# Two hybrid layers on one core: the last batch in halves of positions, its gated jobs in tiles, and query projections moved ahead

## The chip, the core and the metric

The kernel runs on one core of a Trainium2 chip. Its engines each work through an instruction queue of their own, in order, and wait for one another by semaphores: PE (TensorE, matrix multiplication and transposes through it), DVE (VectorE), ACT (ScalarE), POOL (GpSimd), and SP, which here only issues DMAs. Matrix results land in PSUM, in banks of 128 partitions by 512 float32; everything else lies in SBUF.

The metric is the device time of one launch in microseconds (us), as the median of several runs. The profile is one further execution, recorded by the hardware profiler. Its "span" is the time from the first to the last instruction.

## What is computed

The input x has 4 batches of 512 positions and 256 features, all in float32. Four blocks follow each other, each added to x:

```python
x = x + _L0_attn_a_ref(_layernorm(x), ...)   # full attention, 16 heads of 128
x = x + _L0_ffn_ref(_layernorm(x), ...)      # gated job, below
x = x + _L0_attn_b_ref(_layernorm(x), ...)   # low-rank attention, 16 heads
x = x + _L0_ffn_ref(_layernorm(x), ...)      # gated job again
```

The low-rank attention compresses x to 64 columns, projects queries (and a rotary part of 64) from them, scores causally, and multiplies back:

```python
q = x @ Wqa @ Wqb;  ckv = x @ Wkva
attn = softmax(where(causal, concat(q_nope, rope(q_pe)) @ concat(k_nope, rope(k_pe)).T * scale, min))
out = (attn @ v).reshape(b, n, H * VDIM) @ Wout
```

The gated job (`_L0_ffn_ref`) transposes the first two axes: it runs along the batch index l (4 steps), separately for each of the 512 positions. At step l it needs the normalised x of step l-1 (a convolution of width 2) and the keys and values of all steps up to l, but nothing of other positions:

```python
x = silu(x_prev * conv_w[:, 0] + x * conv_w[:, 1])
q, k, v, g = silu(x @ Wq), x @ Wk, x @ Wv, x @ Wg    # q, k rotated by l
qk = (q_exp @ k_exp.T) * HDK ** -0.5 * tril            # 4 x 4 over l, 16 heads
out = (silu(g) * headwise_norm(qk @ v)) @ Wout
```

## The kernel before

**Tiles and jobs.** A batch of x is four SBUF tiles `x[b][t]` of 128 positions. Two attention loops set the order of the PE work. Beside them run "jobs": Python generators that issue a few instructions and then yield. They stand in two lanes, `norms` (layer norms, L132) and `work` (mainly `gated`, L525), and `beside(times)` (L125) advances them by that many steps, alternating between the lanes. There is no scheduler: the order in which the program issues instructions is the order on each engine. A gated job of one batch is two generators, one for each half (two tiles, `HT` = 2), taken in turn (`in_turn`, L731).

**First attention** (`attention_full`, L180). One unit is one head of one batch: scores (L288), maximum (L296), exponential (L299), division by the sum on POOL (L314), a transpose by way of DRAM (`carry`, L328: one DMA out, four DMAs back, all from SP's queue), values (L350), output projection (L372). In the last units `prologue(i)` and `prologue_end(i)` (L1088, L1109) issue the start of the second attention: stage -3 loads rotary tables and query weights (`load_tables`), stage -2 loads the key weights (`load_keys`) and compresses the queries, stage -1 compresses the keys (L944) and projects query pair 0 (L977), stage 0 projects pairs 1 to 3 (pair 1 already stands at the end of stage -1).

**Second attention** (`attention_lowrank`, L845). One unit is (batch b, octet of heads o, half s of the octet, query tile t): four heads by 128 queries, as four blocks of 32 queries (index i). There are 64 units, 16 to a batch, and t runs fastest: 0, 1, 2, 3. Tile t sees (t+1)*128 keys, so units of t = 2, 3 have wide instructions. `score(u, i)` is one matmul (L1000), the masked maximum on DVE (L1008) and the exponential on ACT (L1011). `divide(u)` is a reciprocal (L1024) and four POOL multiplications (L1027). `turn(u, k)` is four PE transposes (L1035), whose copy out is on ACT (L1044), or on DVE for k = 1 of the wide units (L1042). `values(u, k)` multiplies by the values (L1059). `output(b, o, t)` projects four heads back and adds to x (L1079, L1086). `project` fills `queries` for one head pair: two matmuls, two DVE products, a shuffle, two ACT copies and two POOL additions (`rotated`, L906).

In the loop (L1120) unit u's slot i holds, in this order, values of unit u-3, score of unit u, turns of unit u-2 and, in slot 0, the division of unit u-1; then projections and outputs at fixed places, and last

```python
                    beside(beside_at[j % NT][i] * (1 if b < B - 1 else 2))
```

which is 16 steps for four units, and 32 in the last batch.

**The gated jobs' places.** `during_lowrank` (L1200) adds the norm and the gated job of batch b-1 (second layer) in unit 4 of batch b. After the loop, L1214 empties the lanes. Then the norm of batch 3 (all four tiles) runs, and its gated job as two halves in turn, each output tile stored by a DMA (L1216 to L1218).

Of the kernel before, what the change touches and what calls it, by code (L numbers as in the profile page):

```python
# [19 lines left out]
P = 128  # L20
# [16 lines left out]
def network(ctx: ExitStack, tc: tile.TileContext, ins: dict, out: bass.AP):  # L37
# [94 lines left out]
    def norm(b, take, extra=None):  # L132
# [3 lines left out]
        for t in range(NT):  # L136
            nc.vector.bn_stats(stats[:, t, :], x[b][t])
            nc.vector.bn_aggr(mv[:, t, :], stats[:, t, :])
            yield
        rstd = lnpool.tile([P, NT], F32, name="rstd")  # L140
        nc.gpsimd.tensor_scalar(rstd, mv[:, :, 1], EPS, None, ALU.add)
        nc.gpsimd.tensor_tensor(rstd, rstd, minus_half[:, :NT], ALU.pow)
        shift = lnpool.tile([P, NT], F32, name="shift")
        nc.gpsimd.tensor_tensor(shift, mv[:, :, 0], rstd, ALU.mult)
        nc.gpsimd.tensor_scalar(shift, shift, -1.0, 1.0, ALU.mult, ALU.mult)
        yield
        yield
        xT = new_xT()
# [15 lines left out]
        for t in range(0, NT, 2):  # L164
            normed = [normalise(t), normalise(t + 1)]
            if extra and t + 2 == NT:
                extra()
            yield
            for i in range(2):
                transpose(t + i, normed[i])  # L170
            yield
# [353 lines left out]
    def gated(layer, l, xT, xT_before, half, after):  # L525


        tiles = range(half * HT, (half + 1) * HT)
        rows = slice(half * HT * P, (half + 1) * HT * P)

        def little(name, cols, tag=None):
            return gpool.tile([P, cols], F32, tag=f"{tag or name}_{half}", name=name)


        cx = wide("cx", half).rearrange("p (c s) -> p c s", c=DC)
# [11 lines left out]
        th = wide("w0", half, "th").rearrange("p (c s) -> p c s", c=DC)  # L547
# [4 lines left out]
        q = wide("q", half).rearrange("p (t k) -> p t k", t=HT)  # L552
        kv = wide(f"kv{l}", half, "kv").rearrange("p (t k) -> p t k", t=HT)
        gd = wide("gd", half).rearrange("p (t k) -> p t k", t=HT)
        for i in range(HT):
# [19 lines left out]
        def rotate(a):  # L575

            qk = a.rearrange("p t (a f j) -> p t a f j", f=2, j=HDK // 2)
            part = [P, HT, H, HDK // 2]
# [4 lines left out]
            size = HT * H * HDK // 2  # L583
            tmp = [
                turn_tmp[:, i * size : (i + 1) * size].rearrange("p (t a j) -> p t a j", t=HT, a=H)
# [12 lines left out]
        thq = wide("w0", half, "thq", HT * DK).rearrange("p (t k) -> p t k", t=HT)  # L598
        thg = wide("w1", half, "thg").rearrange("p (t v) -> p t v", t=HT)
        nc.scalar.activation(thq, q, AF.Tanh, scale=0.5)  # L600


        r = little("r", HT * H, f"r{l}")
        by_tile = [r[:, i * H : (i + 1) * H] for i in range(HT)]
        nc.vector.tensor_scalar(r.rearrange("p (t h) -> p t h", t=HT), dl, -(2.0**-25), None, ALU.is_ge)
        history[layer, l, half] = kv, r
        gap = little("gap", HT * H)
        nc.vector.scalar_tensor_tensor(
            gap.rearrange("p (t h) -> p t h", t=HT), dl, -1.0, dl, ALU.mult, ALU.max
# [4 lines left out]
        e = gpool.tile([P, B, HT * H], F32, tag=f"e_{half}", name="e")  # L614
        for m in range(l + 1):
            nc.vector.tensor_tensor(e[:, m], r, history[layer, m, half][1], ALU.is_equal)
# [7 lines left out]
        count = little("count", HT * H)  # L624
        if l:
            nc.vector.tensor_reduce(count, e[:, : l + 1].rearrange("p m h -> p h m"), AX.X, ALU.add)
        else:
# [11 lines left out]
            e[:, : l + 1], e[:, : l + 1], gap.unsqueeze(1).to_broadcast([P, l + 1, HT * H]), ALU.mult  # L639
# [4 lines left out]
        a = gpool.tile([P, B, HT * H], F32, tag=f"a_{half}", name="a")  # L644
        prod = wide("w0", half, "prod").rearrange("p (i t k) -> p i t k", i=2, t=HT)
        for m in range(l + 1):
            nc.vector.tensor_tensor(prod[:, m % 2], q, history[layer, m, half][0][:, :, :DK], ALU.mult)
            nc.vector.tensor_reduce(
                a[:, m], prod[:, m % 2].rearrange("p t (h d) -> p (t h) d", d=HDK), AX.X, ALU.add
            )  # L650
            yield
        nc.vector.tensor_tensor(a[:, : l + 1], a[:, : l + 1], e[:, : l + 1], ALU.mult)
        yield
        o = wide("cx", half, "o").rearrange("p (t v) -> p t v", t=HT)
        part = [o] + [
            wide(f"w{i}", half, "part").rearrange("p (t v) -> p t v", t=HT) for i in range(min(l, 2))
        ]

        def weigh(engine, to, m):
            engine.tensor_tensor(  # L660
                to.rearrange("p t (h d) -> p t h d", d=HDV),
                history[layer, m, half][0][:, :, DK:].rearrange("p t (h d) -> p t h d", d=HDV),
                a[:, m].rearrange("p (t h) -> p t h", t=HT).unsqueeze(3).to_broadcast([P, HT, H, HDV]),
# [20 lines left out]
        sq = wide("w0", half, "sq").rearrange("p (n d) -> p n d", d=HDV)  # L684
        nc.scalar.activation(sq, og, AF.Square)
        yield
        var = little("var", HT * H)
# [4 lines left out]
        half_var, root = little("half_var", HT * H, "gap"), little("root", HT * H)  # L692
        square = little("square", HT * H, "count")
# [11 lines left out]
        nc.vector.tensor_tensor(og, og, root.unsqueeze(2).to_broadcast([P, HT * H, HDV]), ALU.mult)  # L705
        yield
        oT = wide("w1", half, "oT").rearrange("p (t n) -> p t n", t=HT)
        pt = ps_tp()
        for i in range(HT):
# [135 lines left out]
    def attention_lowrank(xTs, events):  # L845
# [5 lines left out]
        units = [(b, o, s, t) for b, o in octets for s in range(2) for t in range(NT)]  # L851
        n, per_batch = len(units), OCT * 8
# [7 lines left out]
        def load_tables():  # L860
            angles, wq = slot("wv1", "angles"), slot("wv0", "wqb")
            nc.sync.dma_start(angles, tables[:, : 2 * S])
            nc.sync.dma_start(wq, to_queries)
# [3 lines left out]
            lw["wq"] = wq.rearrange("r (o p s k) -> r o p s k", o=OCT, p=4, s=2)  # L867
# [38 lines left out]
        def rotated(first, second, ps):  # L906
# [5 lines left out]
                slot(tag, "turns").rearrange("p (i q) -> p i q", q=32)  # L912
                for tag in ("wq0", "wk1")
# [54 lines left out]
        def project(b, o, p):  # L968

            if p == 0:  # L970
                queries[b, o] = [
                    slot(tag, f"qTb{s}").rearrange("p (i h q) -> p i h q", h=4, q=32)
                    for s, tag in enumerate((("probs0", "queries")[o % 2], f"v{o % 2}"))
# [72 lines left out]
        quads = {}  # L1046
# [3 lines left out]
        def values(u, k):  # L1050
# [15 lines left out]
            if k == t:  # L1066
                if t == 1:
                    quads[b, o, s] = slot(f"zT{1 + u // NT % 3}", "zTb").rearrange(
                        "p (t n) -> p t n", t=NT
                    )  # L1070
                nc.vector.tensor_copy(
                    quads[b, o, s][:, t - 1 : t + 1, :].rearrange("p b n -> p (b n)"), open_bank.pop()
                )

        def output(b, o, t):

            po = ps_mm()
            for i in range(4):
                nc.tensor.matmul(  # L1079
                    po[:, :D],  # L1080
                    lhsT=quads[b, o, i // 2][:, t, (i % 2) * P : (i % 2 + 1) * P],
# [6 lines left out]
        def prologue(i):  # L1088

            stage = i - H * B  # L1090
            if i == H * (B - 1):
                load_first()
            elif stage == -3:
                load_tables()
            elif stage == -2:
                load_keys()
                compress_queries(0)
            elif stage == -1:
                compress_keys(0)
                project(0, 0, 0)()  # L1100
            elif stage == 0:
                buffers()
                halves = [split(f"squares{k}", k) for k in range(2)]
                project(0, 0, 2)()
                probs_of(0, halves)
                probs_of(2, [slot("probs_2", "probs2")])
                probs_of(3, [slot("probs1", "probs3")])

        def prologue_end(i):  # L1109
            if i - H * B in (-1, 0):  # L1110
                project(0, 0, 3 + 2 * (i - H * B))()

        pair_at = {(1, 0): 0, (3, 1): 1, (5, 0): 2, (6, 1): 3}
        output_at = {(1, 1): 0, (1, 3): 1, (3, 0): 2, (3, 3): 3}
# [185 lines left out]
```

## Time and profile before

| what | us |
|---|---|
| median of 3 runs (lowest, highest) | 1459.04 (1457.69, 1462.09) |
| the profiled execution, its own time | 1464.73 |
| its span | 1463.0 |
| PE busy in the span | 1331.4 (91%) |
| DVE busy | 875.0 (60%) |
| ACT busy | 601.8 (41%) |
| POOL busy | 519.1 (35%) |

The second attention starts with the scores at 821.12 us of the span. Its batches begin there and at 964.92, 1097.40 and 1226.94 us. The last x is written by it at 1394.95 us. From there to 1463.0 us only the norm and the gated job of batch 3 run.

In a row of the timeline the first number is the start, the second the duration, both in us; then engine, line, operation, output and inputs with shapes, how many instructions ("x4"). In brackets stands how long the engine was idle before, and what ended the idle time. A float32 matmul is recorded as two passes, so "x8" on PE are four matmuls.

### The profile page before, as it was taken

What the parts mean: (1) busy time and instruction counts of PE and PEld (TensorE: products, weight loads), DVE (VectorE), ACT (ScalarE), POOL (GpSimd) and SP (SyncE); (2) the same over time, 40 slices, a digit from 0 to 9 for tenths busy, and PEclk for the clock granted to TensorE, in tenths of its full rate; (3) what the DMA queues carried; (4) which work ended last, traced back from release to release, by engine and by line L of the source; (5) the groups of instructions that cost most, each with busy time, mean ns of one, the idle gap of its engine ahead of it and who ended that gap; (6) DMA issues with size and microseconds to landing.
All of it is one profiled execution on the core that took longest, in us unless ns stands there. A gap on an engine that the chain in (4) does not pass through costs nothing.

```text
span 1463.0 us, 17042 instructions
## 1 busy us (share of the span) xinstructions
PE 1331.4 (91%) x4984; PEld 768.1 (53%) x4984; DVE 875.0 (60%) x2634; ACT 601.8 (41%) x1654; POOL 519.1 (35%) x907
## 2 busy tenths in 40 slices
PE   7989999999999999999998789988999999788852
PEld 3445555555656555565554555544555555445531
DVE  3544454553665647655467655698566765867537
ACT  3433333343343343333333246455565645453420
POOL 2311112221232223312144435575353535645333
PEclk9999999999999999999999799999999999898975
DMA  3686655643554445545344200000000000000000
GB/s 112 177 252 191 183 165 183 194 144 119 173 166 147 139 121 157 175 136 169 115 141 147 65 15 1 1 1 1 1 1 1 1 11 4 1 15 1 15 0 14
DMA packets 88140, 133.80 MB, mean 91 GB/s; under 512 B 16112, under 2 KB 69872, under 8 KB 88048
## 3 DMA queue, kind: packets, MB, share of 16 engines
q1 hardware_dynamic: 88048, 132.72, 30.5%
q8 instruction: 40, 0.66, 0.2%
q14 instruction: 52, 0.43, 0.1%
HBM read 86.29 MB, written 46.40 MB: 91 GB/s over the span
## 4 chain that ended last, share of the span: by engine, by line
PE 72%; DVE 13%; POOL 5%; ACT 4%; DMA 3%; issue 2%; SPq 1%; ACTq 0%; DVEq 0%; POOLq 0%
PE ps_mm L262 14%; PE ps_pz L350 8%; PE ps_sc L288 8%; PE ps_mm L249 7%; PE ps_mm L372 7%; PE ps_mm L559 6%; PE ps_sc L1000 5%; PE ps_pz L1059 4%; PE ps_mm L1079 3%; PE ps_tp L1035 3%; PE ps_mm L719 2%; DVE ps_sc L1008 2%; DMA way<-squares 2%; PE ps_mm L977 1%; POOL probs L1027 1%
## 5 line engine op out<-in xcount | busy, mean ns | idle before, releaser
L314 POOL TENSOR_SCALAR probs<-probs,inv 128x128 f32<-128x128 f32 (+3 forms) x256 | 135.1, 546 | 549.7 <-DVE inv L311 487.5
L299 ACT ACTIVATE probs<-ps_sc,nmax 128x128 f32<-128x128 f32 (+3 forms) x256 | 135.0, 528 | 268.6 <-DVE nmax L296 268.1
L1000 PE MATMUL ps_sc<-kTb,qTb 128*128 128x160 f32 (+15 forms) x512 | 175.5, 437 | 11.7 <-POOL qTb L923 5.1
L1011 ACT ACTIVATE probs<-ps_sc,nmax 128x160 f32<-128x160 f32 (+2 forms) x192 | 104.0, 542 | 199.1 <-DVE nmax L1008 138.3
L1008 DVE CUSTOM_DVE_ANT_0 ps_sc<-ps_sc,mask_b 128x32 f32<-128x32 f32 (+15 forms) x256 | 112.9, 444 | 91.4 <-PE ps_sc L1000 70.5
L288 PE MATMUL ps_sc<-kT,qT 128*128 128x128 f32 (+3 forms) x512 | 159.3, 434 | 1.9 <-DVE kT L276 0.9
L296 DVE CUSTOM_DVE_ANT_0 ps_sc<-ps_sc,mask_a 128x128 f32<-128x128 f32 (+3 forms) x256 | 126.3, 499 | 41.9 <-PE ps_sc L288 40.7
L350 PE MATMUL ps_pz<-probsT,v 128*128 128x512 f32 (+3 forms) x512 | 151.1, 438 | 0.0
L1027 POOL TENSOR_SCALAR probs<-probs,inv 128x160 f32<-128x160 f32 (+2 forms) x192 | 107.9, 580 | 109.5 <-DVE inv L1024 78.7
L1000 PEld LDWEIGHTS ps_sc<-kTb,qTb 128*128 128x128 f32 x512 | 84.8, 199 | 105.9 <-issue 58.9
L350 PEld LDWEIGHTS ps_pz<-probsT,v 128*128 128x128 f32 x512 | 97.6, 192 | 79.2 <-issue 58.2
L363 DVE TENSOR_SCALAR zT<-ps_pz,bias 128x512 f32<-128x512 f32 x64 | 48.0, 751 | 144.7 <-PE ps_pz L350 144.7
L262 PE MATMUL ps_mm<-xT,wk 128*128 128x512 f32 x256 | 124.3, 609 | 8.7 <-DMA wk<-in_a_wk_dram 8.5
L249 PE MATMUL ps_mm<-wv,xT 128*128 128x512 f32 x256 | 121.8, 601 | 0.0
L372 PE MATMUL ps_mm<-wo,zT 128*128 128x256 f32 x512 | 121.0, 380 | 0.0
L262 PE MATMUL ps_mm<-xT,wq 128*128 128x512 f32 x256 | 120.3, 592 | 0.0
L323 DVE STREAM_TRANSPOSE squares<-probs 128x512 f32<-128x512 f32 (+3 forms) x256 | 115.1, 487 | 0.0
L1035 PE MATMUL ps_tp<-ident,probs 128*128 128x128 f32 x576 | 93.8, 286 | 19.8 <-ACT probsT L1044 10.7
L288 PEld LDWEIGHTS ps_sc<-kT,qT 128*128 128x128 f32 x512 | 86.6, 190 | 39.2 <-issue 31.0
L256 ACT COPY v<-ps_mm 128x512 f32<-128x512 f32 x64 | 37.5, 586 | 165.1 <-PE ps_mm L249 165.1
L372 PEld LDWEIGHTS ps_mm<-wo,zT 128*128 128x128 f32 x512 | 93.7, 190 | 16.2 <-issue 4.9
L559 PE MATMUL ps_mm<-w_in,cx 128*128 128x512 f32 (+1 forms) x256 | 94.5, 505 | 5.5 <-DVE cx L550 4.2
(150 smaller groups left out, 2058.4 us busy)
## 6 DMA issues: line engine op xcount, KB each, us to landing
way<-squares SPq DMA_DIRECT2D x64, 640.0 KB, 2.9
probsT<-way SPq DMA_DIRECT2D x256, 160.0 KB, 3.3
wv<-in_a_wv_dram SPq DMA_DIRECT2D x16, 512.0 KB, 5.3
wq<-in_a_wq_dram SPq DMA_DIRECT2D x32, 256.0 KB, 3.9
wk<-in_a_wk_dram SPq DMA_DIRECT2D x32, 256.0 KB, 3.9
wo<-in_a_wo_dram SPq DMA_DIRECT2D x16, 512.0 KB, 4.9
x<-in_x_dram SPq DMA_DIRECT2D x16, 128.0 KB, 3.5
out_dram<-x SPq DMA_DIRECT2D x16, 128.0 KB, 1.7
```

What stands on the lines that cost most here:

```text
L249: nc.tensor.matmul(pv, lhsT=xTs[b][:, c, t * P : (t + 1) * P], rhs=wv[g][:, c, :], start=(c == 0), stop=(c == DC - 1),)
L262: nc.tensor.matmul(ps, lhsT=w[u // 2][:, c, (u % 2) * DH : (u % 2 + 1) * DH], rhs=xTs[b][:, c, :], start=(c == 0), stop=(c == DC - 1),)
L288: nc.tensor.matmul(ps[:, :m], lhsT=queries[u][:, t * P : (t + 1) * P], rhs=keys[u][:, :m], start=True, stop=True,)
L296: nc.vector.tensor_tensor_reduce(ps[:, :m], ps[:, :m], mask[:, S - m :], -1.0, 3.0e38, ALU.add, ALU.min, nmax[:, t : t + 1])
L299: nc.scalar.activation(pr[:, t, :m], ps[:, :m], AF.Exp, bias=nmax[:, t : t + 1], scale=-1.0, accum_out=total[:, t : t + 1],)
L314: nc.gpsimd.tensor_scalar(pr[:, t, :m], pr[:, t, :m], inv[:, t : t + 1], 1.0, ALU.mult, ALU.mult)
L350: nc.tensor.matmul(z[:, :, k:, :], lhsT=v[:, k, j * DH : (j + 1) * DH], rhs=pT[:, :, f : f + m, :], start=(k == 0), stop=(k == NT - 1),)
L372: nc.tensor.matmul(po[:, :D], lhsT=zTs[HG * g + i][:, t].rearrange("p i b -> p (i b)"), rhs=wo[g][:, i, :], start=(i == 0), stop=(i == HG ...
L559: nc.tensor.matmul(ps[:, : hi - lo], lhsT=cx[:, c, i * P : (i + 1) * P], rhs=w_in[:, c, lo:hi], start=(c == 0), stop=(c == DC - 1),)
L1000: nc.tensor.matmul(ps, lhsT=q[:, m // 32 - 1].rearrange("p h q -> p (h q)"), rhs=kT[:, :m], start=True, stop=True,)
L1008: nc.vector.tensor_tensor_reduce(ps, ps, lw["mask"][:, S - m :], -1.0, 3.0e38, ALU.add, ALU.min, nmax[:, i : i + 1])
L1035: nc.tensor.transpose(pt.rearrange("p (h i q) -> p h i q", h=4, i=4)[:, :, i, :], lw["probs"][t][i][:, k * P : (k + 1) * P], ident,)
```

## The change

1. **Order of the last batch.** Its 16 units are sorted: first the eight with t = 0, 1 (256 positions, all heads), then the eight with t = 2, 3. In this batch turns and values follow their scores sooner, and outputs and projections have new places. `quads`, the buffers that collect values, are now one for each pair of tiles of an octet, and not one for each half of its heads.
2. **Gated job of batch 3 split.** The norm and the gated job of its tiles 0 and 1 enter the lanes in unit 10 of the last batch; tiles 2 and 3 follow after the loop, each tile a generator of its own, the two in turn. `norm` and `gated` take a list of tiles. Before, each generator held two tiles.
3. **More steps beside the loop.** `beside_at` has 19 steps for four units in place of 16; in the last batch there are 2 in each slot of the first eight units, 3 in the others.
4. **Second attention's start.** The queries are compressed one stage earlier and projected at stages -2, -2, -1 and 0. The query weights are loaded at stage -4, the rotary tables at -3, the key weights at -1 (before: -2); the key compression moves from the middle of stage -1 to its end. The octets' query buffers swap places.

```diff
@@ norm, gated
-    def norm(b, take, extra=None):
+    def norm(b, take, extra=None, tiles=range(NT), xT=None):
-    def gated(layer, l, xT, xT_before, half, after):
-        tiles = range(half * HT, (half + 1) * HT)
+    def gated(layer, l, xT, xT_before, tiles, half, after):
+        nt, place = len(tiles), tiles[0] // HT
+        rows = slice(tiles[0] * P, (tiles[-1] + 1) * P)
+        first = tiles[0] % HT
+        def past(m):
+            kv, r = history[layer, m, place]
+            return kv[:, first : first + nt, :], r[:, first * H : (first + nt) * H]
...
@@ attention_lowrank
         units = [(b, o, s, t) for b, o in octets for s in range(2) for t in range(NT)]
+        units.sort(key=lambda unit: (unit[0], unit[0] == B - 1 and unit[3] // 2))
...
-                for tag in ("wq0", "wk1")
+                for tag in ("wq0", lw["turn"])
-                    for s, tag in enumerate((("probs0", "queries")[o % 2], f"v{o % 2}"))
+                    for s, tag in enumerate((("queries", "probs0")[o % 2], f"v{o % 2}"))
...
-                if t == 1:
-                    quads[b, o, s] = slot(f"zT{1 + u // NT % 3}", "zTb").rearrange(
+                if s == 0:
+                    quads[b, o, t // 2] = slot(f"zT{1 + next(turns) % 3}", "zTb").rearrange(
...
@@ prologue, prologue_end
+            elif stage == -4:
+                load_queries()
             elif stage == -3:
-                load_tables()
+                load_angles()
+                compress_queries(0)
             elif stage == -2:
-                load_keys()
-                compress_queries(0)
+                lw["turn"] = "probs_2"
+                project(0, 0, 0)()
             elif stage == -1:
-                compress_keys(0)
-                project(0, 0, 0)()
+                load_keys()
+                project(0, 0, 2)()
             elif stage == 0:
+                project(0, 0, 3)()
                 buffers()
...
+            if stage == -2:
+                project(0, 0, 1)()
             elif stage == -1:
+                compress_keys(0)
...
@@ places in the loop
+        for u, (b, o, s, t) in enumerate(units):
+            for k in range(t + 1):
+                if b < B - 1:
+                    turns_of[u + 2][k].append((turn, (u, k)))
+                elif t < 2:
+                    first[u + 2][0].append((turn, (u, k)))
+                else:
+                    j, i = ((1, 2), (1, 3), (2, 0), (2, 0))[k]
+                    first[u + j][i].append((turn, (u, k)))
+                if t % 2:
+                    j, i = (3, k) if b < B - 1 else (2, 1) if t < 2 else (2, (0, 0, 1, 2)[k])
+                    first[u + j][i].append((values, (u, k)))
...
+            if b + 1 < B:
+                places = (9, 1), (9, 3), (11, 0), (11, 3)
+            elif o == 0:
+                places = (7, 1), (7, 3), (14, 1), (14, 3)
+            else:
+                places = (1, 2), (1, 3), (9, 2), (9, 3)
+            for t, (j, i) in enumerate(places):
+                at(u + j, i, output, b, o, t)
...
-        beside_at = ((0, 1, 0, 1), (1, 1, 1, 1), (1, 1, 1, 1), (1, 2, 1, 2))
+        beside_at = ((1, 1, 0, 1), (1, 1, 1, 1), (1, 2, 1, 1), (1, 2, 2, 2))
...
-                    beside(beside_at[j % NT][i] * (1 if b < B - 1 else 2))
+                    beside(beside_at[units[u][3]][i] if b < B - 1 else 3 if jb > 7 else 2)
...
@@ the last gated jobs
+    def last_half(xT):
+        gated_in[1][B - 1] = xT
+        work.add(gated(1, B - 1, xT, gated_in[1][B - 2], HALVES[0], 0, store))
+    def last_quarters(xT):
+        jobs = [gated(1, B - 1, xT, gated_in[1][B - 2], [t], t % 2, store) for t in HALVES[1]]
+        work.add(in_turn(*jobs))
...
+        if (b, jb) == (B - 1, 10):
+            norms.add(norm(B - 1, last_half, tiles=HALVES[0]))
...
+    while norms.jobs:
+        beside()
+    norms.add(norm(B - 1, last_quarters, tiles=HALVES[1], xT=gated_in[1][B - 1]))
     while norms.jobs or work.jobs:
-        beside()
-    run(norm(B - 1, then_gated(1, B - 1, store)))
-    while work.jobs:
         beside()
```

In the order of instructions that the changed program issues, the half job of tiles 0 and 1 has its input matmuls in unit 60 and its output matmuls in unit 62 of the 64. The gated job of batch 2 moves up with the denser steps: its input matmuls from units 56 and 57 to 54 and 55, its output matmuls from 62 and 63 to 59. That of batch 1 moves from units 47 and 48 to 40 to 42, and from 55 to 49.

## The prediction

> **What bounds the kernel now.** I read the slices first, then busy time by stage, then the timelines of the two places that the change touches.
>
> ```profile
> PE   7989999999999999999998789988999999788852
> PEclk9999999999999999999999799999999999898975
> ```
>
> Each digit is a fortieth (36.6 us). TensorE is nearly full, with three weak places: around 800 us (digits 22 and 23: the second attention starts), the last batch of that attention (from digit 35), and the end. Busy time in the last batch (1227 to 1395), in the end behind its last add, and in two places inside the batch:
>
> ```profile
> core 0: us, PE busy (x) PEld busy (x) DVE busy (x) ACT busy (x) POOL busy (x), PEclk, DMA share, GB/s
> 1227.00:1395.00 168.00, 144.88 (x650) 86.23 (x648) 112.48 (x354) 75.95 (x219) 81.72 (x142) 0.93 0.02 7
> 1395.00:1463.00 68.00, 23.33 (x64) 13.95 (x64) 39.03 (x102) 12.52 (x30) 23.11 (x38) 0.65 0.02 8
> 1265.80:1283.00 17.20, 11.13 (x58) 7.20 (x56) 15.92 (x54) 7.47 (x23) 9.72 (x13) 0.80 0.00 1
> 1342.80:1360.50 17.70, 10.88 (x54) 7.67 (x53) 15.83 (x42) 6.43 (x21) 11.79 (x14) 0.71 0.00 0
> ```
>
> The last batch is TensorE's (86%), but in the two short windows VectorE is busy 90% and TensorE 63%. The end, 68 us, is a chain: no engine is full, and TensorE's part shows its shape.
>
> ```profile
> 1406.01 13.26 PE L559 MATMUL ps_mm<-w_in,cx 128*128 128x512 f32 x32 [2.88 <-DVE cx L550]
> 1452.23 1.97 PE L711 MATMUL ps_tp<-ident,o 128*128 128x128 f32 x8 [32.96 <-DVE o L705]
> 1454.07 5.86 PE L719 MATMUL ps_mm<-w_out,oT 128*128 128x256 f32 x16
> ```
>
> Columns: start, length, engine and work, and in brackets the idle time before and who ended it. The middle of the end is 33 us in which TensorE waits for VectorE's gated work. And the start of the second attention:
>
> ```profile
> 803.67 3.33 PE L977 MATMUL ps_mm<-qa,wqb 64*128 64x512 f32 x4 [2.30 <-DVE x L379]
> ...
> 814.86 1.12 PE L977 MATMUL ps_mm<-qa,wqb 64*128 64x512 f32 x2 [1.26 <-ACT qTb L918]
> 821.12 1.12 PE L1000 MATMUL ps_sc<-kTb,qTb 128*128 128x32 f32 x4 [5.14 <-POOL qTb L923]
> ```
>
> Here TensorE projects queries, waits for their turning, and last waits 5.14 us for POOL before the first score.
>
> All sums are against the profiled execution: span 1463.0, own time 1464.73 (1.7 around it). The median of the runs, 1459.04, is 5.7 lower; I carry a difference over to it unscaled.
>
> **1. The end: half the positions are left: -21 us (-14 to -27).** Today it is 1394.95 (last add) to 1463.0.
> (a) Last add to first input matmul: 11.06 us. Two of four pairs of statistics fall away (0.53 us from one to the next: 1.05), and the convolution chain on cx (4.6 us) halves to some 2.4. -3.3 (2 to 4.5).
> (b) L559's 32 passes take 13.26 us: the first five 0.855 each, then 0.43 for 512 columns and 0.24 for the narrower ones. Sixteen are left: 5 x 0.855 + 3 x 0.43 + 8 x 0.24 = 7.5. -5.7.
> The slow passes go with the granted clock, 0.65 over this window. The Trainium skill, "TensorE: Matmul & The Clock Gate", Part 1, says that a cold array needs about 3.4 us of sustained work, time rather than instructions, before it speeds up; by it four slow passes stay in the half job too and the input takes about 7.1 us (an estimate), where halving would say 6.6.
> (c) VectorE from 1419.73 to 1452.23: 32.5 us. It is made of small operations with a fixed part:
>
> ```profile
> L674 DVE TENSOR_TENSOR o<-o,part 128x512 f32<-128x512 f32 x2 | 3.0, 1540 | 0.0
> ...
> L680 DVE TENSOR_TENSOR o<-o,part 128x512 f32<-128x512 f32 x4 | 2.5, 679 | 0.0
> ...
> L703 DVE SCALAR_TENSOR_TENSOR root<-square,root 128x32 f32<-128x32 f32 x6 | 1.2, 192 | 0.2
> ```
>
> (Busy us, mean ns of one, idle before.) Columns that hold positions halve: 512 wide 0.68 goes to 256 wide 0.42; 256 wide 0.42 to 128 wide 0.28. The gates 8.9 to 6.7; eight products with their sums 6.5 to 4.2; output terms 9.05 to 5.7; squares and variance 3 to 1.9; the last product (0.74) to 0.42; the root (32 wide, 3.66 with what stands about it) stays. -9.6 (-5 to -13: nothing but the widest gains, or all halves but the root).
> (d) The end proper, 1452.23 to 1463: half the transposes, 8 of 16 output passes, two of four adds (they end at 1456.2 to 1460.0). -2.6.
> Together -21.2; the two tiles as jobs in turn may hide one another or double the fixed part, which the bounds hold.
>
> **2. The start of the second attention: -4 us (-8 to +3).** TensorE idles about 11 us between 787 and 821. Now tiles 0 and 1's first queries are projected two stages earlier, tile 2's one, and the mix and output (2.16 + 1.73 us) stand between tile 3's projection and the first score, so that POOL's turning has cover: 5.14 goes to about 1.3. The move brings SP's queue with it:
>
> ```profile
> 782.15 1.75 SPq L337 DMA_DIRECT2D probsT<-way  x4
> 784.00 0.38 SPq L871 DMA_DIRECT2D wkv<-tables  x1
> 789.14 0.34 SPq L334 DMA_DIRECT2D way<-squares  x1
> ```
>
> load_keys' wkv now stands behind the carry of unit 62. That unit's turn ends near 795 on VectorE; way lands 3.0 later, four issues take 1.75, wkv lands 3.55 after its own: 803.7. TensorE would want it near 799.5. So about 4.2 us of a new wait, plus some 0.9 and 1 for the copies of the earlier projections and the fourth score of unit 63. My walk through this order puts the first score at 816.5 (was 821.1) and the first maximum, which also waits for a mask, at 818.0 (was 821.8): 4. Bounds: no keys wait at all, -8; keys 4 later still and nothing hidden, +3.
>
> **3. Batches 0 to 2: +6 us (0 to +11).** 19 for 16 steps of side work in four units, 36 more in three batches. This pulls the gated job of batch 1 forward: half of its input matmuls, 5.3 us (8.6 us of warm L559 passes in a whole job, with transposes and copies about 10.6), leave the last batch for these. It is a move, not a gain: -5.3 stands in part 4. Side work is one instruction group a step, in line with attention; 36 more places at which TensorE may wait cost little while VectorE is under 70%. I add 0.7.
>
> **4. The last batch: +10 us (-5 to +30).** Work: the half job brings 16 input passes (8 x 0.43 + 8 x 0.23 = 5.3), 8 output passes at 0.216 (1.7) and transposes (1.2): +8.2, and -5.3 from part 3: +2.9. Outputs of tiles 0 and 1 move from the end of the batch to its middle, the work being the same.
> Waits: units of tiles 0 and 1 for all heads come first, then eight units of tiles 2 and 3 in a row. In those, turn(u, 0) stands in slot 2 of the next unit, some two slots behind its divide; before it was a unit later. The chain behind a unit's first new score is the maximum (0.69), the reciprocal (0.17) and POOL's four multiplications:
>
> ```profile
> 1351.44 3.49 POOL L1027 TENSOR_SCALAR probs<-probs,inv 128x416 f32<-128x416 f32 x4 [0.92 <-DVE inv L1024]
> ...
> 1379.08 2.54 POOL L1027 TENSOR_SCALAR probs<-probs,inv 128x416 f32<-128x416 f32 x4 [4.75 <-DVE inv L1024]
> ```
>
> With 2.5 to 3.5 for POOL that is about 3.7; the scores that TensorE issues meanwhile cover 0.8 (tile 2) to 2.6 us (tile 3). Let w be the wait left per heavy unit: 0 (the half job's matmuls cover it) to 3.7 (nothing does). What queues behind a waiting turn on TensorE is the next scores, and so the next maximum. I take w = 0.9, nearest to the well covered tile 3 unit: 8 x 0.9 = 7. Sum +10.
> The port rule speaks against the change. Row: L674, two inputs, beside POOL's L660, is 1540 ns; L680, same shape, alone, 679. The Trainium skill, "SBUF — State Buffer", Who interferes with whom, says why: VectorE and GpSimd share a port pair as an exclusive lock. Inside the heavy units the half job's wide operations stand beside POOL's divides; some 12 of them x 0.86 are 10 us (an estimate) on VectorE, which by the 112.5 of 168 has 55 us free; by the rule, if all of it showed, the total would be +1.
>
> **Sum:** -21 - 4 + 6 + 10 = -9: 1464.73 to 1455.7 profiled, 1450 on the median's level.
>
> **Rivals.** Measurements of this kernel tell about 0.3% (4.4 us) from no change.
> *R1, the loop hides its waits* (w = 0, part 3 a pure move, end -24): -4 + 5.3 + 2.9 - 24 = -20, time 1439. For: VectorE has room in the batch. Against: VectorE is 90% busy in the light windows, where the half job also goes; a single chain with a hand-off per step.
> *R2, slower: turns right behind their divides.* Everything else nets -16 (the sum without its waits), and each heavy unit pays w: -16 + 8w. It decides from w = 2.6, where the time is 4.4 up; at 3.7 it is +14, 1473. For: the 3.49 us of POOL above, and a turn in that unit already waits 3.6 us. Against: TensorE is 100% busy from 1306 to 1343 in the present heavy units, so there cover is plenty.
> *R3, given back: the change doesn't do what it says.* Keys land so late that the start gains 0; w = 1.5 (12); the end gives only 19: 0 + 6 + 2.9 + 12 - 19 = +2, time 1461. For: the carry's place on SP. Against: 5.14 us is one clear wait that the new order covers.
>
> **How the numbers follow.** Forecast 0.42 (its own range -5 to -14: 1445 to 1454), R1 0.26, R3 0.19, R2 0.13. Faster by over 0.3% are the forecast and R1: 0.68; within, R3: 0.19; slower, R2: 0.13. The range reaches into R1 by a third of the way to its bound (1437) and to R3's far edge (1462), with R2 and the last of R1 left out.
>
> **What would show it.** The time from the last add to the end near 47 (was 68), VectorE's stretch between input matmuls and transposes near 23 (was 32.5); TensorE's wait for POOL before the first score near 1, and a new one of about 4 for wkv at the keys' compression; in the last eight units TensorE waiting at turns for POOL's probabilities, under 1 us each; the last batch about 178 long; the half job's output matmuls issued before the last unit's end. I am wrong if the turns' waits pass 2.6 us a unit, if the end is above 54, or if the first score isn't earlier.

## The result: 4.8% slower, and the loss is in the loop

The changed kernel takes 1530.64 us (median of 4 runs, 1527.12 to 1532.15) against 1460.29 us of the kernel before (4 runs); the ratio is 1.048, 95% interval 1.0453 to 1.0506. The forecast was 1450, with a range to 1462. The profiled execution has a span of 1530.4 us against 1463.0. Cut at the first score of the second attention, at the starts of its batches and at its last add, the 67.4 us lie here:

| stage | before, us | after, us | difference | forecast |
|---|---|---|---|---|
| up to the first score of the second attention | 821.1 | 825.4 | +4.3 | -4 |
| its batches 0 to 2 | 405.8 | 443.1 | +37.3 | +6 |
| its last batch, to the last add | 168.0 | 218.7 | +50.7 | +10 |
| the end behind the last add | 68.0 | 43.2 | -24.8 | -21 |

The end did what it should, and a little more. The loop lost three and a half times as much. The slices of the changed kernel show where; the digits are tenths of a fortieth of the span, now 38.3 us.

```profile
PE   7989999999999999999997889899988897776773
...
PEclk9999999999999999999997999899998999788886
```

From digit 30 on TensorE's nines thin out (before, digits 29 to 34 were all nines), and the granted clock sinks with them. Busy time of batches 0 to 2 together, the kernel before first (start and end, length, then busy us and instructions of each engine, the clock, the DMA):

```profile
core 0: us, PE busy (x) PEld busy (x) DVE busy (x) ACT busy (x) POOL busy (x), PEclk, DMA share, GB/s
821.10:1226.94 405.84, 374.12 (x1708) 216.04 (x1708) 268.41 (x838) 218.93 (x626) 198.68 (x313) 0.98 0.01 5
```

and the changed one, with its last batch and its end:

```profile
825.45:1268.56 443.11, 391.79 (x1725) 224.43 (x1725) 282.39 (x886) 222.67 (x636) 214.26 (x354) 0.95 0.02 7
1268.56:1487.20 218.64, 164.54 (x666) 97.50 (x664) 118.18 (x370) 80.45 (x224) 79.47 (x137) 0.84 0.02 7
1487.20:1530.40 43.20, 13.13 (x32) 7.25 (x32) 24.23 (x96) 7.08 (x21) 14.28 (x38) 0.64 0.02 6
```

Read it in two parts. Idle time of TensorE (length less busy) in batches 0 to 2 went from 31.7 to 51.3 us, in the last batch from 23.1 to 54.1. But TensorE's busy time rose as well, by 17.7 us in batches 0 to 2 for 17 recorded passes more (the moved half of a gated job's input, 5.3 us by the forecast), and by 19.7 in the last batch for 16 passes more, while the clock fell from 0.98 to 0.95 and from 0.93 to 0.84. So a wait can be paid twice: once as idle time, and again in slower matmuls behind it.

The end, as TensorE's timeline shows it (start, length, work, and in brackets the wait before it):

```profile
1494.19 7.05 PE L570 MATMUL ps_mm<-w_in,cx 128*128 128x512 f32 x16 [2.34 <-DVE cx L561]
1522.38 1.11 PE L723 MATMUL ps_tp<-ident,o 128*128 128x128 f32 x4 [21.14 <-DVE o L717]
```

The input's 16 passes take 7.05 us (7.5 was forecast, 13.26 the whole before), and TensorE waits 21.14 us for VectorE, not 32.96.

### The profile page after: what moved, and what is told of

Same layout as the page of the kernel before. It is cut to its first block, busy times and chain, and to the rows that moved or that the text cites. A ratio compares the mean times of both kernels' runs of the same rounds, so it can differ in the third digit from the quotient of the medians.

```text
span 1530.4 us, 17142 instructions
## 1 busy us (share of the span) xinstructions
PE 1360.6 (89%) x4984; PEld 781.7 (51%) x4984; DVE 878.6 (57%) x2678; ACT 604.2 (39%) x1660; POOL 521.5 (34%) x928
## 4 chain that ended last, share of the span: by engine, by line
PE 71%; DVE 12%; POOL 6%; ACT 5%; issue 3%; DMA 2%; SPq 1%; ACTq 0%; POOLq 0%; DVEq 0%
PE ps_mm L265 14%; PE ps_pz L353 8%; PE ps_sc L291 8%; PE ps_mm L252 7%; PE ps_mm L375 7%; PE ps_mm L570 6%; PE ps_sc L1018 5%; PE ps_pz L1077 4%; PE ps_mm L1095 3%; PE ps_tp L1053 3%; PE ps_mm L731 2%; POOL probs L1045 2%; DVE ps_sc L1026 2%; PE ps_mm L995 1%; ACT probs L1029 1%
## 5 line engine op out<-in xcount | busy, mean ns | idle before, releaser
L1018 PE MATMUL ps_sc<-kTb,qTb 128*128 128x160 f32 (+15 forms) x512 | 179.9, 447 | 18.1 <-ACT probs L1029 8.8
L1053 PE MATMUL ps_tp<-ident,probs 128*128 128x128 f32 x576 | 99.2, 294 | 27.0 <-POOL probs L1045 16.0
L570 PE MATMUL ps_mm<-w_in,cx 128*128 128x512 f32 (+1 forms) x256 | 99.7, 525 | 19.3 <-DVE cx L561 15.3
L1053 PEld LDWEIGHTS ps_tp<-ident,probs 128*128 128x128 f32 x576 | 74.8, 152 | 59.6 <-POOL probs L1045 26.0
```

The source lines that it names most:

```text
L570: nc.tensor.matmul(ps[:, : hi - lo], lhsT=cx[:, c, i * P : (i + 1) * P], rhs=w_in[:, c, lo:hi], start=(c == 0), stop=(c == DC - 1),)
L1018: nc.tensor.matmul(ps, lhsT=q[:, m // 32 - 1].rearrange("p h q -> p (h q)"), rhs=kT[:, :m], start=True, stop=True,)
L1053: nc.tensor.transpose(pt.rearrange("p (h i q) -> p h i q", h=4, i=4)[:, :, i, :], lw["probs"][t][i][:, k * P : (k + 1) * P], ident,)
```

## The experiments

Each run gives one profile beside a run of the kernel before on the same chip; e11 and e12 were timed in rounds. Over the kernels with the old table (before, e2, e5, e6, e7, e8, e9, e11, e12) batches 0 to 2 took 402.5 to 407.6 us: differences below 5 us are not read there.

**e1 and e2: the table of side work, alone and undone.**

```diff
 # e1, from the kernel before
-beside(beside_at[j % NT][i] * (1 if b < B - 1 else 2))
+beside(beside_at[j % NT][i] * 2 if b >= B - 1 else ((1, 1, 0, 1), (1, 1, 1, 1), (1, 2, 1, 1), (1, 2, 2, 2))[j % NT][i])
 # e2, from the changed kernel
-beside_at = ((1, 1, 0, 1), (1, 1, 1, 1), (1, 2, 1, 1), (1, 2, 2, 2))
+beside_at = ((0, 1, 0, 1), (1, 1, 1, 1), (1, 1, 1, 1), (1, 2, 1, 2))
```

> The kernel before with one thing of the change alone: the denser table of side work, in batches 0 to 2 of the second attention (the last batch keeps its twofold table). Theory D (the denser side work is what lengthened batches 0 to 2, through TensorE standing at hand-offs of the side jobs and running at a lower granted clock): batches 0 to 2 together go from 405.8 us to 430 to 445, the last batch loses about 5, the total rises by 20 to 35. Theory O (the density is harmless, and the loss comes with the start or with the phase in which the loop enters): batches 0 to 2 stay within 6 us of 405.8 and the total within 6 us of the kernel before.

> The changed kernel with the old, thinner table of side work in batches 0 to 2. Theory D: batches 0 to 2 together go from 443.1 us back to 405 to 420, the last batch grows by about 5 (the moved input matmuls), the total falls by 20 to 35, to about 1502. Theory O: batches 0 to 2 stay above 435 and the total within 6 us of 1530.

Measured: 1493.24 us for e1 (beside 1461.58) and 1488.31 for e2. Batches 0 to 2 in e1 and in e2 (the kernel before and the changed one stand above, with 405.84 and 443.11 us):

```profile
824.10:1266.30 442.20, 393.44 (x1725) 226.02 (x1725) 278.51 (x874) 222.50 (x636) 212.03 (x340) 0.95 0.01 4
```

```profile
823.70:1228.70 405.00, 370.35 (x1708) 213.57 (x1709) 270.98 (x850) 218.33 (x626) 200.10 (x327) 0.99 0.02 7
```

Two kernels at 442 to 443 us, two at 405 to 406: the table alone makes the 37 us, and nothing else in the change matters there beyond the 5 us of scatter. Of it, 9.6 us came back in e1's last batch (158.4 instead of 168.0), where the moved matmuls no longer stand. e2's last batch was expected to grow by about 5 us. It fell from 218.7 to 214.7, so its loss has another source.

Where the idle time is, the waits of TensorE in batches 0 to 2 say (total us, times, longest). Two of the rows that grew most, before and then in the changed kernel:

```profile
PE ps_tp L160 <- ACT xn L152: 6.6, 5, 2.6
...
PE ps_mm L559 <- DVE cx L550: 1.1, 1, 1.1
```

```profile
PE ps_tp L163 <- ACT xn L155: 9.3, 8, 3.2
...
PE ps_mm L570 <- DVE cx L561: 5.1, 2, 2.6
```

Over all rows of the norms' and the gated jobs' own matmuls, TensorE waited 11.9 us in 11 waits before and 23.8 us in 20 waits in the changed kernel; in e1 it was 23.9, in e2 11.9. So 11.9 of the 19.6 us more of idle time stand directly at side work. They are not all waits for a side job's own data: L570's wait for ACT's copies of the queries grew from 1.3 to 4.0 us. The other 7.7 us stand before the attention's own matmuls; whether the side work's lateness is passed on there is not shown.

One such place is in batch 2 of the changed kernel. POOL and ACT and TensorE and VectorE around one norm:

```profile
1164.48 1.08 PE L1077 MATMUL ps_pz<-probsT,probsT 128*64 128x512 f32 x4
...
1169.00 0.20 POOL L148 TENSOR_SCALAR shift<-shift 128x4 f32<-128x4 f32 x1
...
1169.24 1.09 ACT L155 ACTIVATE xn<-x,shift,rstd 128x256 f32<-128x256 f32 x2 [2.35 <-POOL shift L148]
1169.89 0.69 PE L163 MATMUL ps_tp<-ident,xn 128*128 128x128 f32 x2 [3.17 <-ACT xn L155]
...
1171.77 1.98 PE L1077 MATMUL ps_pz<-probsT,probsT 128*64 128x512 f32 x4
...
1175.15 0.50 DVE L1026 CUSTOM_DVE_ANT_0 ps_sc<-ps_sc,mask_b 128x320 f32<-128x320 f32 x1 [4.11 <-PE ps_sc L1018]
...
1178.64 0.93 PE L163 MATMUL ps_tp<-ident,xn 128*128 128x128 f32 x4 [1.89 <-ACT xn L155]
```

Here the norm's steps follow each other faster than POOL, ACT and TensorE hand the data on. ACT waits 2.35 us for POOL, its next exponential queues behind, TensorE's transposes wait 3.17 for ACT with all attention work behind them in order, and the same four passes of L1077 then take 1.98 us instead of 1.08. VectorE idles 4.11 us. From 1166 to 1182 the busiest engine is TensorE with 10.3 of 16 us, VectorE has 3.3: no engine is full, the chain is.

**e10: the same amount of side work, spread evenly.** `beside(1 if b < B - 1 else 2 * beside_at[j % NT][i])` in the kernel before: 16 steps in four units, one in each slot.

> The kernel before with its side work in batches 0 to 2 kept at 16 steps in four units, but one step in every slot, with neither empty nor double slots. Theory A (it is the amount of side work per unit that matters): batches 0 to 2 stay within 8 us of 405. Theory P (it is where the steps stand: by the empty slots of the shortest unit and the double ones of the longest the old table follows the units' own length): they rise by 12 us or more.

Measured: batches 0 to 2 took 410.2 us (+4.4, under the 5 us that are read here). Theory A: at 16 steps the places within a unit hardly matter. What e10 does not move is the unit in which a whole job falls. The denser table moves that too (batch 1's job comes some six units earlier), and no run holds the amount and moves the job, so these two are not told apart.

**e3: the keys' load one stage earlier.**

```diff
 elif stage == -2:
     lw["turn"] = "probs_2"
+    load_keys()
     project(0, 0, 0)()
 elif stage == -1:
-    load_keys()
     project(0, 0, 2)()
```

> The changed kernel with the load of wkv issued one stage earlier, ahead of the carry of unit 62 on SP. If the late load is what the start pays for: TensorE's 4.8 us wait for wkv goes to under 1, the eight matmuls of the keys' compression go from 6.3 us back to about 3.7 (they ran at a lower granted clock behind that wait), the first score comes 6 to 8 us earlier, the total falls by as much. Rival (the copies and turnings of the queries set the first score, the keys only fill that time): the first score comes less than 2 us earlier.

The moment of the first score scatters, 821.2 to 825.4 us over six kernels with the same new start. So I count from the first attention's last projection of values: 62.4 to 63.4 us in the four kernels with the old start (before 62.6); 62.5 to 65.5 in the six with the new one (the changed kernel 65.5, e2 63.1, e4 62.5); 59.8 in e3. The keys' compression in the kernel before:

```profile
787.59 3.70 PE L944 MATMUL ps_mm<-xT,wkv 128*128 128x512 f32 x8 [0.21 <-DMA wkv<-tables]
```

in the changed one:

```profile
809.08 6.33 PE L962 MATMUL ps_mm<-xT,wkv 128*128 128x512 f32 x8 [4.76 <-DMA wkv<-tables]
...
825.45 1.60 PE L1018 MATMUL ps_sc<-kTb,qTb 128*128 128x32 f32 x6 [3.33 <-POOL qTb L941]
```

and in e3:

```profile
802.76 1.88 PE L962 MATMUL ps_mm<-xT,wkv 128*128 128x512 f32 x4
806.20 1.98 PE L962 MATMUL ps_mm<-xT,wkv 128*128 128x512 f32 x4 [1.56 <-DVE x L382]
```

The wait for the DMA is gone, and the eight passes are back at 3.9 us. The first score comes 7.2 us earlier than in the changed kernel (818.23), but by the marker the gain is 2.7 to 5.7 us and in the span 3.9 (1526.5), under the 6 to 8 that I expected: the wait for POOL before the first score stays at 3.3.

**e4 and e5: the last batch without the half job, at the new and at the old density.** Both run the gated job of tiles 0 and 1 behind the loop; e5 has the old table too, doubled in the last batch.

```diff
-if (b, jb) == (B - 1, 10):
-    norms.add(norm(B - 1, last_half, tiles=HALVES[0]))
...
 while norms.jobs:
     beside()
+norms.add(norm(B - 1, last_half, tiles=HALVES[0]))
+while norms.jobs:
+    beside()
 # e5 alone
-beside(beside_at[units[u][3]][i] if b < B - 1 else 3 if jb > 7 else 2)
+beside(beside_at[units[min(u, n - 1)][3]][i] * (1 if b < B - 1 else 2))
```

> The changed kernel with the gated job of tiles 0 and 1 of the last batch taken out of the loop and run behind it, ahead of that of tiles 2 and 3. Theory H (the half job in the loop, a single chain whose hand-offs TensorE waits for, is what lengthened the last batch): the last batch goes from 218.6 us to 175 to 190, the end grows from 43 to about 75, the total moves by less than 12. Rival W (the order of the units, with turns close behind their divides, did it): the last batch stays above 200 and the total rises by 15 or more.

> The changed kernel with the old table of side work everywhere (in the last batch twice that table, as before) and the gated job of tiles 0 and 1 run behind the loop: of the change to the last batch, the order of the units and the places of turns, values and outputs are left. Before, that batch took 168.0 us with this amount of side work. Theory D2 (it is the density of the side work that hurts, by way of a VectorE that runs late; the order costs little): 165 to 178 us. Rival W (the order with turns close behind their divides costs by itself): above 185 us. The end stays near the 81 us of the run with the half job at the end in both, so the total is 1470 to 1482 by D2 and above 1490 by W.

Last batches of e4 and e5, and e5's end:

```profile
1266.80:1458.57 191.77, 150.16 (x634) 89.25 (x632) 100.40 (x319) 74.39 (x209) 68.08 (x116) 0.85 0.02 6
```

```profile
1228.60:1408.16 179.56, 150.63 (x650) 89.56 (x648) 110.20 (x354) 77.66 (x219) 82.87 (x142) 0.90 0.02 7
1408.16:1489.10 80.94, 26.92 (x64) 14.95 (x64) 43.61 (x147) 13.30 (x36) 26.04 (x59) 0.62 0.02 7
```

Neither run fell where one theory had it. e4 (1541.69 us) lies between 190 and 200, e5 (1490.83 us, beside 1463.0) between 178 and 185. Together they split the last batch's +50.7. The new order of units and turns alone costs 11.6 (179.6 less 168.0). The density costs 21.8 by this sum: e4's 191.8, plus the 9.6 that e1 showed to have moved out of the batch, less 179.6. The half job in the loop costs 26.9 (218.7 less 191.8). And 9.6 had moved away. The parts are not independent: e2 has the same last batch with the 9.6 back in it, and took 214.7 where this sum would give 228. Between e4 and the changed kernel the half job is worth its place even so: it takes 38 us from the end (81.4 to 43.2).

**e7: the last batch's density in the old order.** `beside(beside_at[j % NT][i] if b < B - 1 else 3 if jb > 7 else 2)` in the kernel before.

> The kernel before with one thing alone: in the last batch two, and from unit 56 on three, steps of side work a slot in place of twice the old table. Theory D2: the last batch grows from 168.0 us by 8 to 20, with VectorE's maxima late in the units behind 56. Rival W: it stays within 5 us, since the order is the old one.

Measured: 174.3 us for the last batch, +6.3, total 1467.53 beside 1463.0: between the two. In the old order the density costs a third of the 21.8 us that the sum gives for the new one, where the short units of tiles 0 and 1 come together and the three steps a slot fall on the eight heavy units. That this is the reason is argued, not shown.

What happens there is seen in the changed kernel at 1352 to 1382, where VectorE is busy 25.63 of 30.00 us, TensorE 18.65. The lines of four engines around one score, its maximum, its exponential and the copy behind it:

```profile
1355.97 0.91 PE L1018 MATMUL ps_sc<-kTb,qTb 128*128 128x384 f32 x2 [0.38 <-ACT probs L1029]
...
1362.66 0.66 DVE L659 TENSOR_TENSOR prod<-q,kv 128x256 f32<-128x256 f32 x1 [1.47 <-POOL q L605]
...
1364.47 0.56 DVE L1026 CUSTOM_DVE_ANT_0 ps_sc<-ps_sc,mask_b 128x384 f32<-128x384 f32 x1
...
1365.12 0.58 ACT L1029 ACTIVATE probs<-ps_sc,nmax 128x384 f32<-128x384 f32 x1 [3.48 <-DVE nmax L1026]
...
1365.69 1.06 ACT L1062 COPY probsT<-ps_tp 128x512 f32<-128x512 f32 x2
...
1366.32 2.83 PE L1077 MATMUL ps_pz<-probsT,probsT 128*64 128x512 f32 x8 [6.12 <-ACT probsT L1062]
```

The score is done at 1356.9. Its maximum starts at 1364.5, because VectorE's queue holds the gated job's products, and the first of them waits for POOL's rotation of q. ACT's exponential waits for the maximum, the copy of turned probabilities stands behind the exponential, and TensorE waits 6.12 us for the copy. None of the three needed the gated job. This is one chain of several; how much of the batch's loss goes this way was not added up.

**e6 and e8: the half job at the old density, and the turn of block 0 one slot later.** e6 is e5 with the half job in the loop again; e8 changes in it `((1, 2), (1, 3), (2, 0), (2, 0))[k]` to `((1, 3), (1, 3), (2, 0), (2, 0))[k]`.

> As the run before it, but with the gated job of tiles 0 and 1 in the loop again, so that side work comes at the old density everywhere. Theory D2: the last batch falls from the 214.7 us that it took with three steps a slot to 185 to 200 and the end stays near 43, if the half job still ends inside; total 1455 to 1475. Rival H2 (the half job costs its waits wherever it stands in a loop of heavy units): the last batch stays above 208 us.

> As e6_thin_half_job, with one thing moved: in the eight heavy units the turn of block 0 stands one slot later (slot 3 instead of 2 of the next unit), beside that of block 1. In e6 TensorE waited 10.4 us in the last batch at turns for POOL's divided probabilities (longest 5.6), because the reciprocal stood on VectorE behind side work and the next unit's maximum. Theory W (that wait is the price of turns close behind their divides): it falls to under 6 us and the last batch from 186.9 us by 4 to 8. Rival (the wait only moves on to the next score or the values): the batch stays within 2 us of 186.9.

e6: last batch 186.9 us, end 51.8 (its last steps run behind the loop), total 1468.56 beside 1463.0: Theory D2, but for the end. e2 and e6 differ in nothing but the density in the last batch. Their last batches (e2, then e6):

```profile
1228.70:1443.37 214.67, 166.78 (x682) 98.84 (x680) 129.08 (x405) 83.39 (x234) 93.00 (x163) 0.88 0.02 7
```

```profile
1228.10:1414.97 186.87, 154.02 (x670) 93.58 (x668) 125.61 (x387) 82.63 (x232) 93.65 (x162) 0.92 0.02 6
```

So with the half job in the loop the density alone costs 27.8 us there. Up to 8.6 of them are work that e6 leaves to its end (51.8 for 43.2); the totals are 19.8 us apart. In e6 the last batch and the end together take 238.7 us, against 236.0 before: what the end gained is given back in the batch. e8: 184.8 and 53.3, total 1470.35 beside 1460.85. TensorE's waits for POOL's probabilities in the last batch of e6, then of e8 (total us, times, longest):

```profile
PE ps_tp L1053 <- POOL probs L1045: 10.4, 9, 5.6
```

```profile
PE ps_tp L1053 <- POOL probs L1045: 3.1, 6, 1.4
PE ps_tp L1053 <- ACT probsT L1062: 3.0, 1, 3.0
```

The wait that the forecast named is there and goes when the turn moves, by 7.3 us. The batch gains only 2.0: the rest moved on, in part to ACT's copies. So this wait was not the price of the order; what the 11.6 us consist of stays open.

**e11: put right by these runs.** e8, with e3's early keys, and 10 and 12 steps a unit in the last six units meant to let the half job end inside.

> The changed kernel put right by what the runs showed: the old table of side work, wkv loaded one stage earlier, the turns of block 0 one slot later, and in the last six units and behind them 10 and 12 steps of side work a unit, so that the gated job of tiles 0 and 1 ends inside the loop. Theory D2: first score 819, batches 0 to 2 406, last batch 186 to 192, end 43 to 46, span 1454 to 1462: the same as before within what can be told. Rival: the extra steps bring VectorE's lateness back and the last batch stands above 198, span above 1466.

Measured in three rounds: ratio 1.006, interval 1.0042 to 1.0078. The last batch took 198.1 us, the end 48.4, the profiled span 1474.9; the rival's figures. The half job did not end inside even so: its output matmuls start at 1431.5 us, behind the last add at 1426.5. The extra steps made the batch 13 us longer than e8's and brought TensorE a wait of 8.1 us for ACT's copies at 1371.5; at 1362.8, shortly before, VectorE had waited 2.95 us for POOL's part of the gated job.

**e9 and e12: the new start alone.** The kernel before with the start of the changed one and e3's early keys.

> The kernel before with the new start alone, and with the load of wkv one stage earlier as in e3_keys_early. From the last projection of values of the first attention to the first score of the second it took 62.6 us in the kernel before, 65.5 in the changed one and 59.8 in e3. Theory S (the new start is right and only the late keys spoil it): 59 to 61 us here, and the total 1 to 4 us under the kernel before. Rival: the gain in e3 came from the rest of the changed kernel, and here it is 62 or more.

> The kernel of e9_start_alone, for its interval. Theory S: its start saves about 4 us of 1460, a ratio of 0.997 whose interval may just reach 1. Rival: the saving in the one profile was chance, and the ratio is 1.000 or above.

Measured: 58.3 us from the last projection of values to the first score (62.6 before), e9 as a whole 1460.09 beside 1460.85; in e12's five rounds a ratio of 0.9967, interval 0.9955 to 0.9979 (1459.66 against 1464.63 us). This version is faster than both kernels. The rest of the loop is that of before.

## Why the prediction was wrong

**Step 1, the end: right.** -24.8 against -21 (-14 to -27). Last add to first input matmul -4.1 (forecast -3.3), input passes -6.2 (-5.7), VectorE's stretch 32.5 to 21.7, -10.8 (-9.6), the output part -2.8 (-2.6), and 1.0 because VectorE's stretch now begins shortly before the last input pass ends and before began behind it. The mechanism held as well as the number, though the terms given for VectorE's stretch add up to 9.3 and not to 9.6.

**Step 2, the start: the wait was found, its consequence was not.** -4 was forecast, and the first score came 4.3 us later; by the marker the new start costs 1.0 us in the mean of six profiles against four, so the gain did not come. The wait for wkv was named with 4.2 us and came with 4.76. Two terms were missing: the eight passes behind it at the lower clock (6.33 for 3.70 us), and POOL's turning, which kept 3.33 us of the 5.14 where 1.3 was forecast. e9 shows -4.3 when the keys come early.

**Step 3, batches 0 to 2: the step that failed.** "36 more places at which TensorE may wait cost little while VectorE is under 70%. I add 0.7." With the move of 5.3 that made +6; it was +37, as e1 and e2 show each for itself, so the 0.7 became about 32. The condition held (VectorE 64%, 282 of 443 us) and the conclusion did not follow: 11.9 us of the new waits stand at the side jobs' own matmuls, which stand in order between those of the attention, and wait for what another engine has to hand on. VectorE's average did not show them. About 12 us more are the clock's, as reckoned below. How near the edge the old table stood is not known: nothing was run between 16 and 19 steps. (The 8.6 us for a whole job's input passes do not fit part 4's rows, which give twice 5.3; the 5.3 that was used is right by them.)

**Step 4, the last batch: it failed too, by a missing term and one that was too small.** It was put at +10, at most +30, and came to +50.7. Turns behind their divides were put at w = 0.9; waits at turns for POOL's probabilities were 12.0 us in the changed kernel, 1.5 for each of eight units. But by e8 most of such a wait only moves on when the turn is later. The half job was priced at its matmuls, 8.2 us, and cost 26.9 in place, at this density; at the old one 7.3 (e6 less e5), with some of it behind the loop. The density itself had no term; it cost 21.8 by the sum, and by e2 and e6 27.8 in the batch, 19.8 in the total. R2 was the rival with the right sign and the wrong mechanism: its price per unit stayed under the 2.6 us from which it decides. Of the three signs of being wrong only the first score's came; none of them watched the density.

**The clock had no term at all.** In the last batch of the changed kernel, two groups of the same eight input passes of the half job:

```profile
1414.95 4.70 PE L570 MATMUL ps_mm<-w_in,cx 128*128 128x512 f32 x8 [5.88 <-DVE cx L561]
...
1420.51 2.80 PE L570 MATMUL ps_mm<-w_in,cx 128*128 128x512 f32 x8
```

and the granted clock of these two stretches (the value before the DMA's):

```profile
1414.95:1419.60 4.65, 4.65 (x10) 2.38 (x11) 0.00 (x0) 0.65 (x2) 0.00 (x0) 0.61 0.00 0
1420.50:1423.30 2.80, 2.80 (x11) 1.62 (x10) 0.59 (x2) 1.55 (x5) 0.00 (x0) 1.00 0.02 6
```

0.61 behind a wait of 5.88 us, 1.00 a moment later: the wait costs 1.9 us more than itself (4.70 for 2.80). The prediction reckoned with slow passes in the end and not in the loop. The Trainium skill, "TensorE: Matmul & The Clock Gate", Part 1, has the array fall back to half clock after an idle window of about 3.4 us; this row agrees, and the longest waits of the last batch (5 to 6 us) are of that kind. In batches 0 to 2 no wait is longer than 3.3 us and the clock still fell to 0.95, so there shorter ones were enough: the wait of 3.17 us that ends at 1169.89 runs into a granted clock of 0.50 (1169.42 to 1176.24), and the one of 1.89 us that ends at 1178.64 is followed by 0.50 again (1179.66 to 1183.07). No run holds the clock while the waits stay, so its share is read from rows and not from an experiment: busy time less the work moved in is about 12 us in batches 0 to 2 (17.7 less 5.3), and in the last batch about 16: 164.5 x 0.84 is 138, 144.9 x 0.93 is 135, so in clocked work the two batches differ by 3 of the 19.7 us.

Rows that fit the port rule that was weighed stand in the loop: in the changed kernel L686, two inputs and 512 wide, took 1.54 us at 1374.32, beside POOL's L672, and 0.68 at 1376.69 with POOL idle. POOL's four divisions of 416 columns took 3.50 us in one unit of e6 (1340.68) and 2.53 in one of the changed kernel (1382.74). What it adds in all was not measured by itself.

## What to carry to other kernels

Side work that is threaded through a full engine's loop can be too dense well before any engine is full: here 19 steps in four units cost 37 us in batches 0 to 2 where 16 stood before, with VectorE at 64%. As far as the rows show, what counts is the time that one step's data needs to pass from engine to engine until the next step is issued, and neither engine averages nor the side job's own busy time show it. Before the density is raised, look for the side job's matmuls that already wait in the present trace, and count each wait of TensorE by its length and by the slower matmuls behind it. A change with several parts should be run part by part: here one part, put right, gains 0.3% by itself, one gains 25 us at the end and, in every version of it that was run, lost at least as much in the last batch, and a table of sixteen small numbers loses 37.

## What was not expected of the hardware

TensorE's clock answered to waits well under the longest one in the profile: with nothing above 3.3 us in batches 0 to 2, the same four passes went from 1.08 to 1.98 us, and a wait of 1.89 us was followed by 3.4 us at a granted clock of 0.50. In a stretch where no engine is above 65% busy, the loop ran at 0.71 of TensorE's full clock (1166 to 1182).
